# Four graph layers in one kernel: later layers' weights prepared in the second stage, constants made first, first-stage blocks waiting for nodes only

## The chip, the cores and the metric

The kernel runs on one core of a Trainium2 chip. The metric is the device time of one execution in microseconds (us). Every engine of the core works through its own instruction list in order: TensorE (PE, with its weight loads shown apart as PEld), VectorE (DVE), ScalarE (ACT), GpSimd (POOL), and SyncE (SP), whose list issues most of the transfers.

## What is computed

The input is `x`, 128 graphs of 128 nodes with 128 channels, and `adj`, a 0/1 matrix of each graph. Four layers follow one another, each `x = x + layer(relu(layernorm(x)), adj)`. The first layer decides the order of the work:

```
D = jnp.abs(x[:, :, None, :] - x[:, None, :, :])        # every pair of nodes
h = jnp.einsum('bijc,oc->bijo', D, W1) + b1
m = jnp.mean(h, axis=(0, 1, 2)); v = jnp.mean((h - m) ** 2, axis=(0, 1, 2))
h = leaky((h - m) / jnp.sqrt(v + EPS) * g1 + be1)       # then W2, mask, softmax, y, its own norm
```

The mean and variance run over all pairs of all graphs, so they must be known before any edge score can be finished. Layers 1 to 3 are attention layers over the same graphs, with weights of their own (`L1_gnn_*`, `L2_gnn_*`, `L3_gnn_*`); products of these weights (`fw`, `w2g`, `aq`, `aqb`, `a1bc`, `vpw`, `pb_bc` and some masks) are prepared once.

## The kernel before, in words

There are three stages. **First stage**, `statistics()`: for every pair of nodes of every graph it forms |difference|, multiplies by W1 and sums the results and their squares. **Second stage**, `edge_attention()`: it computes the edge scores of the neighbours only, softmax and `y` for 32 groups of four graphs. **Third stage**, `layers()`: the other three layers, group by group.

The first stage treats 32 groups of four graphs. `nodes(g)` (from L613) loads a group (L618), normalises it (DVE L623/L624, ACT L628/L629, POOL L632/L633), transposes it (PE L638), applies relu into `he` (ACT L641), copies a few columns (POOL L644) and then makes `us` (PE L653, ACT L656/L660, DVE L658/L662), three bf16 parts of W1 times the nodes. A graph is cut into four blocks, `block(b, q)` (from L687): a tile `d` of 32 x 64 pairs is made by DVE (L701) or POOL (L706), ACT takes its absolute value (L710), PE multiplies it with W1 (L727), and the result is reduced by DVE (L739) or by ACT (L733). Two of a group's sixteen blocks, called larger, take a maximum in place of the difference, need no ACT step, and add on PE three products of `us` with a constant tile `both`. Nine `d` buffers and three PSUM buffers `ph` are shared by all.

The constants and the later layers' weights are prepared in generators that run among the first blocks: `own_and_later` makes `both` (POOL L590, DVE L595), `first_weight` the transposed W1 (`w1T`, `w1T2`), `attention_weights` `fw` (L323 to L329), `w2g` (L337 to L340) and small masks (L342 to L364), `square_weights` `vpw` and `pb_row` (L385 to L389), `aT` (DVE L398), `aq` (PE L404, ACT L408) and `aqb` (PE L412, DVE L414), and `edge_constants` the constants of the second stage (POOL L419/L423, DVE L429 to L452). Their inputs are loaded by SP near the start (L282 to L299).

Nothing in the two stages runs in the order of the text. Each generator announces its next step with an engine, a cost and the buffers it takes:

```
yield "after", ("nodes", g)
yield DVE, 0.33, "", "ph"
```

The planner `in_order` (from L66) takes the makers in a list, keeps at most eight of them under way in the first stage and nine in the second, and picks the step that can begin first by its own clock. What it picks becomes the fixed instruction order of PE, ACT, DVE and POOL. `begun` gives the clocks at which the engines are thought to begin. A step after `"wait"` becomes due that much later, one after `"after"` when an event is done. In this kernel `("nodes", g)` is announced after `us`, so that no block of a group is placed before the group's `us`.

Of the kernel before, what the change touches and what calls it, by code (L numbers as in the profile page):

```python
# [19 lines left out]
P = 128  # L20
# [153 lines left out]
def kernel(ctx: ExitStack, tc: tile.TileContext, x, adj, w, out):  # L174
# [108 lines left out]
    a1b = w_tile("a1b", [P, NH, 2 * DH])  # L283
    nc.sync.dma_start(a1b, bcast(w["L1_gnn_a1"], 0, P))
    nc.sync.dma_start(w2g[:, :, 0:P], w["L1_gnn_W2"].rearrange("(s k) c -> k s c", k=P))
    a2b = w_tile("a2b", [P, 2, P])
    nc.sync.dma_start(a2b, bcast(w["L1_gnn_a2"].rearrange("(s c) -> s c", s=2), 0, P))
    araw = w_tile("araw", [P, P, NT])
    nc.sync.dma_start(araw, w["L3_gnn_a"])
    raw("qw", w["L3_gnn_qw"], nc.sync)  # L290
    raw("vw", w["L3_gnn_vw"], nc.sync)
    acol = w_tile("acol", [P, 1])
    nc.sync.dma_start(acol, w["L2_gnn_a1"])
# [24 lines left out]
    far = mid_of("far", [P, 1])  # L318

    def attention_weights():  # L320
        yield "wait", 20.0
        yield DVE, 2.9, "", ""
        nc.vector.memset(fw, 0.0)  # L323
        for m in range(2):
            prod = wl.tile([P, NH, DH], F32, tag="prod", name="prod", bufs=2)
            nc.vector.tensor_tensor(prod, w1c, a1b[:, :, m * DH : (m + 1) * DH], ALU.mult)
            sums = wl.tile([P, 2, HH], F32, tag="wsums", name="wsums", bufs=2)
            nc.vector.tensor_reduce(sums.rearrange("p s h -> p (s h)"), prod, AX.X, ALU.add)
            nc.vector.tensor_copy(  # L329
                fw[:, :, 3 * HH * m : 3 * HH * (m + 1)].rearrange("p s (k h) -> p s k h", h=HH),  # L330
                bcast(sums, 2, 3),
            )
        yield "wait", 3.0
        yield DVE, 1.9, "", ""
        for s in range(2):
            prod2 = wl.tile([P, 2, P], F32, tag="prod2", name="prod2", bufs=2)
            nc.vector.tensor_tensor(prod2, w2g[:, :, 0:P], bcast(a2b[:, s, :], 1, 2), ALU.mult)  # L337
            gw = wl.tile([P, 2], F32, tag="gw", name="gw", bufs=2)
            nc.vector.tensor_reduce(gw, prod2, AX.X, ALU.add)
            nc.vector.tensor_copy(w2g[:, :, P + s], gw)  # L340
        yield DVE, 1.3, "", ""
        nc.vector.tensor_scalar(ident_far, ident, FAR, None, ALU.mult)  # L342
        of_32 = w_tile("of_32", [P, 32])
        nc.vector.tensor_reduce(of_32, ident.rearrange("p (g k) -> p k g", k=32), AX.X, ALU.add)
        for m, dst in ((0, of_f1), (1, of_f2)):
            rows = of_32[:, 3 * HH * m : 3 * HH * (m + 1)]
            nc.vector.tensor_reduce(
                dst[:, 0:HH], rows.rearrange("p (k h) -> p h k", h=HH), AX.X, ALU.add
            )
            nc.vector.tensor_reduce(dst[:, HH : HH + 1], rows, AX.X, ALU.add)  # L350
        of_part = w_tile("of_part", [P, 3])
# [7 lines left out]
        yield DVE, 0.8, "", ""  # L359
        nc.vector.tensor_copy(a1bc, acol.to_broadcast([P, P]))  # L360
        hid = w_tile("hid", [P, P])
        nc.vector.tensor_scalar(hid, ident, 0.5, None, ALU.mult)
        for s in range(2):
            nc.vector.tensor_tensor(  # L364
                q_avg[:, s * 64 : s * 64 + 64], hid[:, 0:64], hid[:, 64:128], ALU.add
            )

    def square_weights(psum2):
        yield "wait", 8.0
# [8 lines left out]
        yield "wait", 12.0  # L378
# [5 lines left out]
        yield DVE, 0.7, "", ""  # L384
        nc.vector.tensor_copy(vpw, pvw)  # L385
        nc.vector.tensor_tensor(pb_row, pb_row, pvb, ALU.add)
        nc.vector.tensor_scalar(pb_row, pb_row, -2.0, None, ALU.add)
        ones_row = w_tile("ones_row", [1, P])
        nc.vector.memset(ones_row, 1.0)  # L389
# [5 lines left out]
        aT = w_tile("aT", [P, NT, P])  # L395
        for t in range(0, NT, 2):
            yield DVE, 0.32, "", ""
            nc.vector.tensor_copy(  # L398
                aT[:, t : t + 2, :], araw[:, :, t : t + 2].rearrange("d e t -> d t e")
            )  # L400
        yield PE, 2.1, "ph", ""
        pq = psum2("aq_ps")
        for s in range(2):
            nc.tensor.matmul(  # L404
                pq[:, s, :], raws["qw"], aT[:, 4 * s : 4 * s + 4, :], start=True, stop=True
            )
        yield ACT, 1.1, "", "ph"
        nc.scalar.copy(aq.rearrange("p t e -> p (t e)"), pq.rearrange("p s n -> p (s n)"))  # L408
        yield PE, 2.0, "ph", ""
        pqb = psum2("aqb_ps")[:, 0, 0:NT]  # L410
        for t in range(NT):
            nc.tensor.matmul(pqb[:, t : t + 1], aT[:, t, :], qb, start=True, stop=True)  # L412
        yield DVE, 0.2, "", "ph"
        nc.vector.tensor_copy(aqb, pqb)  # L414

    def edge_constants():
        yield "wait", 30.0
        yield POOL, 0.6, "", ""
        nc.gpsimd.iota(  # L419
            off, pattern=[[1, P]], base=0, channel_multiplier=-1,  # L420
            allow_small_or_imprecise_dtypes=True,
        )
        nc.gpsimd.iota(  # L423
            at, pattern=[[1, P]], base=0, channel_multiplier=0,
            allow_small_or_imprecise_dtypes=True,
        )
        yield DVE, 1.5, "", ""
        tmp = w_tile("tmp", [P, P])
        nc.vector.tensor_scalar(tmp, off, 64.0, None, ALU.is_le)  # L429
        nc.vector.scalar_tensor_tensor(tmp, off, 1.0, tmp, ALU.is_ge, ALU.mult)  # L430
        nc.vector.scalar_tensor_tensor(in_half, off, -65.0, tmp, ALU.is_le, ALU.add)
        nc.vector.tensor_scalar(tmp, ident, -1.0, 1.0, ALU.mult, ALU.add)
        nc.vector.tensor_tensor(in_other, tmp, in_half, ALU.subtract)
        nc.vector.tensor_copy(not_own, tmp)
        yield DVE, 1.3, "", ""
        nc.vector.tensor_scalar(upto, off, 0.0, None, ALU.is_ge)
        back = w_tile("back", [P, P])
        nc.vector.tensor_scalar(back, at, -1.0, P - 1.0, ALU.mult, ALU.add)
        nc.vector.tensor_tensor(tmp, back, ident, ALU.mult)
        nc.vector.tensor_reduce(down, tmp, AX.X, ALU.add)  # L440
        nc.vector.tensor_copy(down_d, tmp)
        yield DVE, 1.1, "", ""
        nc.vector.tensor_copy(ident_h, ident)
        nc.vector.memset(ones, 1.0)
        nc.vector.memset(all_p, float(P))
        nc.vector.tensor_scalar(ident5, ident, 5.0, None, ALU.mult)
        nc.vector.tensor_scalar(ident4, ident, -4.0, None, ALU.mult)
        yield DVE, 1.0, "", ""
        nc.vector.tensor_scalar(least, at[:, 0 : len(SLOTS)], float(P), float(P), ALU.mult, ALU.add)
        for k, n in enumerate(SLOTS):  # L450
            nc.vector.memset(room[:, k : k + 1], float(n))
        nc.vector.memset(far, NEG)  # L452
# [113 lines left out]
    def statistics():  # L566
# [3 lines left out]
        with tc.tile_pool(name="a2", bufs=2) as a2, tc.tile_pool(  # L570
# [17 lines left out]
            def own_and_later():  # L588
                yield POOL, 3.9, "", ""
                nc.gpsimd.tensor_tensor(  # L590
                    both.rearrange("p (i j) -> p i j", j=64),
                    shifted(ident[:, 1:65], QR), bcast(ident[:, 0:QR], 2, 64), ALU.add,
                )
                yield DVE, 0.68, "", ""
                nc.vector.tensor_scalar(both, both, -1.0, None, ALU.mult)  # L595
                yield "done", "both"

            def first_weight():
                yield "wait", 4.0
# [9 lines left out]
            def nodes(g):  # L609

                b0 = g * GB
                if g < len(raw_x):
                    xg = raw_x[g]  # L613
                    yield "wait", 4.0 + 1.2 * g
                else:
                    yield DMA, 0.6, "xg", ""
                    xg = a2.tile([P, GB, P], F32, tag="xg", name="xg")
                    nc.sync.dma_start(xg, x_t[:, b0 : b0 + GB, :])  # L618
# [27 lines left out]

                if g == 0:
# [15 lines left out]
                ready[g] = he, pt, us  # L663
                yield "done", ("nodes", g)
# [17 lines left out]
            def block(b, q):  # L682
# [11 lines left out]
                he, pt, us = ready[g]  # L694
                hb, hp, us = he[:, i, :], pt[:, i, :], us[:, :, i, :]
# [12 lines left out]
                if not is_larger:  # L708
# [4 lines left out]
                    )  # L713
                yield PE, 3.17 if is_larger else 1.76, "ph", "d"
                ph = a_ph.tile([P, 2, 512], F32, tag="ph", name="ph")
# [25 lines left out]
            ready, left, six = {}, [GB] * n_parts, {}  # L741
# [3 lines left out]
            def others():  # L745
                yield "fork", own_and_later()
                yield "fork", first_weight()
                yield "fork", attention_weights()
# [4 lines left out]
            makers = [partial(nodes, 0), others]  # L753
# [5 lines left out]
            begun = dict.fromkeys(AFTER, 1.0) | {POOL: 1.5, ACT: 5.0, DMA: 22.0}  # L759
# [67 lines left out]
    def edge_attention(free_at, banks, total):  # L827
# [3 lines left out]
        with tc.tile_pool(name="b2", bufs=2) as b2p, tc.tile_pool(name="b3", bufs=B_W) as b3p, tc.tile_pool(  # L831
            name="b_ps", bufs=6, space=PSUM
        ) as b_ps, tc.tile_pool(name="b_pq", bufs=1, space=PSUM) as b_pq:
# [336 lines left out]
            makers = [partial(total, psum, own_d), *(partial(group, g) for g in range(n_parts))]  # L1170
# [1340 lines left out]
```

## Time and profile before

| what | value |
|---|---|
| median of 3 runs | 2699.19 us (2699.1 to 2699.64) |
| profiled execution, its own time | 2704.5 us |
| its span | 2702.7 us |
| DVE begins the second stage (L770) | 1101.6 us after the span's start |
| second stage's last group | 1759.0 us |
| mean granted TensorE clock | 0.965 |

| busy over the span | PE | PEld | DVE | ACT | POOL |
|---|---|---|---|---|---|
| us | 2498.0 | 1558.9 | 2437.8 | 2160.7 | 1632.8 |
| share | 92% | 58% | 90% | 80% | 60% |

Shares over the span mix three stages with different limits, so they are read by stretches of time. A line of the timeline gives start, duration, engine, source line, operation, output and inputs with their shapes, how many instructions were merged, and in brackets the idle time before with what ended it. A line of the stretches gives its length, then the busy time of PE, PEld, DVE, ACT and POOL with the number of instructions, the granted TensorE clock, the busy share of the DMA engines and GB/s.

### The profile page before, as it was taken

The numbers are of one execution on the slowest core, as the hardware profiler recorded it, in microseconds if no ns is written. First come the engines' busy times: TensorE is split into PE (matmuls) and PEld (weight loads), VectorE is DVE, ScalarE is ACT, GpSimd is POOL, SyncE is SP. The second block draws the span as 40 slices with busy tenths as digits, with TensorE's granted clock in tenths as the row PEclk, the third lists the DMA queues.
The fourth block names the chain that finished last, engine by engine and source line by source line (L and its number), as shares of the span: only waits on it lengthen the run. The fifth ranks groups of instructions, "written<-read, shape, count | busy, mean of one in ns | idle before, by whom it ended". The sixth has DMA issues, their size and how long they took to land.

```text
span 2702.7 us, 51582 instructions
## 1 busy us (share of the span) xinstructions
PE 2498.0 (92%) x19584; PEld 1558.9 (58%) x19595; DVE 2437.8 (90%) x4648; ACT 2160.7 (80%) x3527; POOL 1632.8 (60%) x923
## 2 busy tenths in 40 slices
PE   6999999999999999799999999868988989898888
PEld 2333444333433333477777777756776767667666
DVE  7999999999999999788899998678988888889886
ACT  4899999999999999566666666568787877787885
POOL 6899999999999999644344444022433333323234
PEclk8999999999999999899999999979999999999999
DMA  3100000000000000322223321040211111111001
GB/s 88 32 24 24 24 24 24 30 26 24 24 24 28 24 20 8 102 88 91 85 85 101 93 81 50 17 137 5 62 36 47 37 44 44 45 38 31 10 2 33
DMA packets 135732, 122.62 MB, mean 45 GB/s; under 512 B 10866, under 2 KB 102451, under 8 KB 135475
## 3 DMA queue, kind: packets, MB, share of 16 engines
q1 hardware_dynamic: 134754, 118.89, 14.4%
q8 instruction: 158, 2.59, 0.4%
q14 instruction: 100, 0.81, 0.1%
q10 hardware_dynamic: 720, 0.33, 0.0%
HBM read 73.05 MB, written 46.14 MB: 44 GB/s over the span
## 4 chain that ended last, share of the span: by engine, by line
PE 45%; DVE 30%; ACT 14%; issue 6%; POOL 2%; DMA 1%; SPq 0%; ACTq 0%; DVEq 0%; POOLq 0%
PE ph L727 13%; DVE d L701 6%; ACT d L710 6%; DVE six L739 5%; PE pl L1056 4%; PE diff L1001 4%; DVE p L1752 3%; PE ph L1014 2%; PE sp L1024 2%; PE po L1709 2%; ACT ph L733 2%; PE va L1781 1%; DVE s L1640 1%; PE ph L1911 1%; PE sm L1781 1%
## 5 line engine op out<-in xcount | busy, mean ns | idle before, releaser
L706 POOL TENSOR_TENSOR d<-he 128x2016 f32<-128x2016 f32 (+1 forms) x272 | 960.7, 3564 | 14.3 <-PE ph L727 8.8
L727 PE MATMUL ph<-d,w1T 128*64 128x512 f32 (+1 forms) x4096 | 919.8, 599 | 37.7 <-DVE six L739 25.0
L710 ACT ACTIVATE d<-d 128x2048 f32<-128x2048 f32 (+1 forms) x448 | 831.8, 1888 | 21.2 <-POOL d L706 14.3
L727 PEld LDWEIGHTS ph<-d,w1T 128*64 128x64 f32 x4096 | 320.7, 137 | 566.8 <-issue 489.1
L701 DVE SCALAR_TENSOR_TENSOR d<-pt,he 128x2048 f32<-128x2048 f32 x240 | 541.5, 2270 | 1.4 <-PE ph L727 1.4
L739 DVE BATCH_NORM_STATS2 six<-ph 128x6 f32<-128x512 f32 (+1 forms) x704 | 436.1, 676 | 16.3 <-PE ph L727 15.1
L1649 POOL TENSOR_TENSOR xn<-xo,mv 128x512 f32<-128x512 f32 x64 | 74.0, 1157 | 324.0 <-DVE mv L1642 256.5
L733 ACT ACTIVATE ph<-ph 128x1008 f32<-128x1008 f32 x160 | 159.6, 997 | 20.7 <-PE ph L727 19.0
L1056 PE MATMUL pl<-its,it 128*128 128x128 f32 x1280 | 171.2, 283 | 0.5 <-DVE its L1049 0.4
L1056 PEld LDWEIGHTS pl<-its,it 128*128 128x128 f32 x1280 | 157.0, 196 | 17.8 <-DVE its L1049 5.8
L1010 ACT ACTIVATE d<-diff 128x640 f32<-128x640 f32 x128 | 89.8, 702 | 91.0 <-PE diff L1001 91.0
L1752 DVE SCALAR_TENSOR_TENSOR p<-z,mask 128x1024 f32<-128x1024 f32 x124 | 147.7, 1210 | 8.0 <-ACT z L1750 7.7
L988 POOL TENSOR_TENSOR base<-base,own_d 128x512 f32<-128x512 f32 x32 | 42.7, 1334 | 179.8 <-PE ph L1014 124.0
L1650 POOL TENSOR_TENSOR xn<-xn,rs 128x512 f32<-128x512 f32 x96 | 111.0, 1156 | 52.9 <-ACT rs L1646 40.8
L1001 PE MATMUL diff<-inc,h 128*128 128x320 bf16 x768 | 128.8, 304 | 3.9 <-DVE inc L917 3.9
L1750 ACT ACTIVATE z<-z 128x1024 f32<-128x1024 f32 x128 | 129.0, 1008 | 4.1
L1046 ACT CAST it<-pi 128x640 f32<-128x640 bf16 x128 | 86.3, 690 | 54.5 <-PE pi L1043 54.5
L917 DVE SCALAR_TENSOR_TENSOR inc<-in_row,row 128x8 bf16<-128x8 f32 (+12 forms) x512 | 126.5, 315 | 0.8 <-PE in_row L908 0.8
L1649 POOL TENSOR_TENSOR xn<-x,mv 128x512 f32<-128x512 f32 x32 | 36.1, 1129 | 136.8 <-DVE mv L1642 73.7
L1781 PE MATMUL va<-p,vals 128*32 128x128 f32 x2048 | 108.7, 285 | 8.3 <-DVE vals L1766 8.1
L1018 ACT ACTIVATE z<-ph,h_bi,h_sc 128x320 f32<-128x320 f32 x128 | 77.9, 618 | 45.0 <-PE ph L1014 43.3
L1997 POOL TENSOR_TENSOR xh<-xh,xo 128x512 f32<-128x512 f32 x32 | 46.9, 1467 | 106.6 <-DVE xh L1718 82.8
(329 smaller groups left out, 5383.9 us busy)
## 6 DMA issues: line engine op xcount, KB each, us to landing
ht<-h SPq DMA_DIRECT2D x64, 256.0 KB, 2.8
n<-ln_xn SPq DMA_DIRECT2D x32, 256.0 KB, 2.4
h<-he SPq DMA_DIRECT2D x32, 256.0 KB, 2.6
adj<-in_adj SPq DMA_DIRECT2D x32, 256.0 KB, 3.0
xn<-n SPq DMA_DIRECT2D x32, 256.0 KB, 2.8
xb<-in_x SPq DMA_DIRECT2D x32, 256.0 KB, 2.9
xb<-xb SPq DMA_DIRECT2D x32, 256.0 KB, 2.0
xg<-xb SPq DMA_DIRECT2D x32, 256.0 KB, 2.7
```

The lines of the kernel that those rows point to most:

```text
L701: nc.vector.scalar_tensor_tensor(dv, own, 0.0, later, ALU.max, ALU.max if is_larger else ALU.subtract)
L706: nc.gpsimd.tensor_tensor(dv, later, own, ALU.subtract)
L710: nc.scalar.activation(d[:, 0 : 4 * n], d[:, 0 : 4 * n], AF.Abs, accum_out=sums[:, g, k : k + 1] if on_act else None,)
L727: nc.tensor.matmul(ph[64 * a : 64 * a + 64, t, 0:n], wt, x_, start=part == 0, stop=not is_larger or part == 3,)
L733: nc.scalar.activation(ph[:, :, 0:n], ph[:, :, 0:n], AF.Square, accum_out=squares[:, g, k : k + 1])
L739: nc.vector.bn_stats(six[g][:, 2 * by_bn.index((i, q)) + t, :], ph[:, t, 0:n])
L917: nc.vector.scalar_tensor_tensor(inc[:, :, e : e + n], in_row[:, :, 0:n], float(k + 1), row[:, :, 0:n], ALU.is_equal, ALU.subtract,)
L1001: nc.tensor.matmul(diff[:, a, 0 : SLOT_N // 2], h[:, i, :], inc[:, a * SLOT_N // 2 : (a + 1) * SLOT_N // 2], start=m == 0, stop=m == 2,)
L1056: nc.tensor.matmul(made["pl"][:, i, :], it[:, k, :], its[:, k, :], start=k == 0, stop=k == 4)
L1750: nc.scalar.activation(z, z, AF.Exp, scale=1.0 - SLOPE)
L1752: nc.vector.scalar_tensor_tensor(p, z, 1.0, bcast(mask[:, i, :], 1, NH), ALU.max, ALU.mult)
L1781: nc.tensor.matmul(to[rows, a, s, :], vals[:, NH * a + e, :] if to is va else es[:, i, e : e + 1].to_broadcast([P, DH]), ps_[i][:, e, :], ...
```

## The change

Three things are done. First, `attention_weights` and the `aT`, `aq`, `aqb` part of `square_weights` become one generator, `layer_weights`, which is placed after 20 of the 32 group makers of the second stage; its steps are cut into smaller ones, its loads (`araw`, `qw`, `a1b`, `acol`, `a2b`) move there too, and four large tiles share two buffers. Second, the constants are placed first: `others` stands ahead of `nodes(0)`, many memsets and both iotas are issued before the planner, scaled copies of the identity and three more copies go to ACT, and `both` is made by one DVE instruction from a negated identity rather than by POOL and DVE. Third, `("nodes", g)` is announced once `he` is complete; `("us", g)` is a second event that only the larger blocks wait for, ahead of their PE step. The estimates in `begun` and some `"wait"` values change as well.

```diff
-    a1b = w_tile("a1b", [P, NH, 2 * DH])
-    nc.sync.dma_start(a1b, bcast(w["L1_gnn_a1"], 0, P))
...
+    minus_ident = w_tile("minus_ident", [P, P])
+
+    def scaled_idents():
+        yield ACT, 0.3, "", ""
+        nc.scalar.mul(minus_ident, ident, -1.0)
+        yield "done", "minus"
+        for dst, factor in ((ident_h, 1.0), (ident5, 5.0), (ident4, -4.0)):
+            yield ACT, 0.27, "", ""
+            nc.scalar.mul(dst, ident, factor)
+        yield ACT, 0.27, "", ""
+        nc.scalar.activation(not_own, ident, AF.Identity, bias=one, scale=-1.0)
+        yield "done", "not_own"
...
+        nc.vector.tensor_scalar(back, at, -1.0, P - 1.0, ALU.mult, ALU.add)
+        yield DVE, 0.29, "", ""
+        nc.vector.tensor_tensor(tmp, back, ident, ALU.mult)
+        yield ACT, 0.27, "", ""
+        nc.scalar.copy(down_d, tmp)
...
+        nc.vector.tensor_tensor(hid, ident[:, 0:64], ident[:, 64:128], ALU.add)
+        yield ACT, 0.5, "", ""
+        for s in range(2):
+            nc.scalar.mul(q_avg[:, s * 64 : s * 64 + 64], hid, 0.5)
+
+    def layer_weights(pool, psum):
+        def big(shape):
+            return pool.tile(shape, F32, tag="big", name="big", bufs=2)
+
+        yield DMA, 0.3, "", ""
+        araw = big([P, P, NT])
+        nc.sync.dma_start(araw, w["L3_gnn_a"])
+        qw = pool.tile([P, P], F32, tag="qw", name="qw")
+        nc.sync.dma_start(qw, w["L3_gnn_qw"])
+        yield "wait", 4.0
+        aT = big([P, NT, P])
+        for t in range(0, NT, 2):
+            yield DVE, 0.4, "", ""
+            nc.vector.tensor_copy(
+                aT[:, t : t + 2, :], araw[:, :, t : t + 2].rearrange("d e t -> d t e")
+            )
+        for s in range(2):
+            yield PE, 1.05, "p", ""
+            pq = psum("aq_ps")
+            nc.tensor.matmul(pq, qw, aT[:, 4 * s : 4 * s + 4, :], start=True, stop=True)
+            yield ACT, 0.58, "", "p"
+            nc.scalar.copy(aq[:, 4 * s : 4 * s + 4, :], pq)
...
-        yield DVE, 0.7, "", ""
-        nc.vector.tensor_copy(vpw, pvw)
-        nc.vector.tensor_tensor(pb_row, pb_row, pvb, ALU.add)
-        nc.vector.tensor_scalar(pb_row, pb_row, -2.0, None, ALU.add)
-        ones_row = w_tile("ones_row", [1, P])
-        nc.vector.memset(ones_row, 1.0)
+        yield ACT, 0.28, "", ""
+        nc.scalar.copy(vpw, pvw)
+        yield DVE, 0.3, "", ""
+        nc.vector.scalar_tensor_tensor(pb_row, pvb, -2.0, pb_row, ALU.add, ALU.add)
...
             def own_and_later():
-                yield POOL, 3.9, "", ""
-                nc.gpsimd.tensor_tensor(
+                yield "after", "minus"
+                yield DVE, 2.3, "", ""
+                nc.vector.tensor_tensor(
                     both.rearrange("p (i j) -> p i j", j=64),
-                    shifted(ident[:, 1:65], QR), bcast(ident[:, 0:QR], 2, 64), ALU.add,
+                    shifted(minus_ident[:, 1:65], QR), bcast(minus_ident[:, 0:QR], 2, 64), ALU.add,
                 )
-                yield DVE, 0.68, "", ""
-                nc.vector.tensor_scalar(both, both, -1.0, None, ALU.mult)
...
+                ready[g] = he, pt
+                yield "done", ("nodes", g)
...
-                ready[g] = he, pt, us
-                yield "done", ("nodes", g)
+                parts_of[g] = us
+                yield "done", ("us", g)
...
+                yield "after", ("us" if is_larger else "nodes", g)
+                if g == 0:
+                    yield "after", "w1"
                 yield PE, 3.17 if is_larger else 1.76, "ph", "d"
...
-            makers = [partial(nodes, 0), others]
+            makers = [others, partial(nodes, 0)]
...
-            begun = dict.fromkeys(AFTER, 1.0) | {POOL: 1.5, ACT: 5.0, DMA: 22.0}
+            begun = dict.fromkeys(AFTER, 1.0) | {POOL: 1.9, ACT: 1.8, DVE: 1.6, DMA: 22.0}
...
+            groups = [partial(group, g) for g in range(n_parts)]
+            weights = partial(layer_weights, w_late, psum)
+            makers = [partial(total, psum, own_d), *groups[:20], weights, *groups[20:]]
```

The rest of `layer_weights` holds the former instructions for `fw`, `w2g`, `a1bc`, `ident_far`, `of_f1`, `of_f2` and `parts_m`, each group behind a smaller `yield DVE`; `a1b` and `a2b` are loaded by SP just ahead of their use.

## The prediction

> **What bounds the kernel now.** I read the stretches of the span first, to find a stage that is not full, then the timeline of DVE and POOL there, then the waits. Stretches (length, then PE, PEld, DVE, ACT, POOL, clock):
>
> ```profile
> 0.00:100.00 100.00, 71.65 (x303) 30.22 (x305) 84.37 (x164) 55.20 (x65) 66.78 (x34) 0.86 0.26 73
> 100.00:1085.00 985.00, 965.56 (x4892) 386.40 (x4890) 971.59 (x1201) 964.21 (x1011) 967.26 (x343) 1.00 0.08 24
> 1400.00:1550.00 150.00, 148.29 (x1324) 116.16 (x1324) 137.38 (x360) 99.78 (x214) 64.45 (x60) 1.00 0.29 90
> ```
>
> From 100 us to the end of the first stage four engines are 98 to 99% busy: no edit to one engine's work there can gain much. The first 100 us are another matter: POOL is busy for 67 of them, ACT for 55. In the second stage PE sets the pace (98.9%), with DVE at 92% and POOL at 43%.
>
> Timeline of DVE, then of POOL, in the poor stretch:
>
> ```profile
> 20.55 3.02 DVE L326 TENSOR_TENSOR prod<-w1c,a1b 128x256 f32<-128x256 f32 x1
> 24.05 2.95 DVE L329 COPY fw<-wsums 128x24 f32<-128x24 f32 x1
> 26.92 0.41 DVE L326 TENSOR_TENSOR prod<-w1c,a1b 128x256 f32<-128x256 f32 x1
> 27.82 2.95 DVE L329 COPY fw<-wsums 128x24 f32<-128x24 f32 x1
> 38.96 2.94 DVE L340 COPY w2g<-gw 128x2 f32<-128x2 f32 x1
> 42.72 3.53 DVE L340 COPY w2g<-gw 128x2 f32<-128x2 f32 x1
> 47.56 0.15 DVE L357 COPY parts_m<-of_part 128x1 f32<-128x1 f32 x1
> ```
> ```profile
> 12.71 18.03 POOL L706 TENSOR_TENSOR d<-he 128x2016 f32<-128x2016 f32 x5
> 31.09 10.79 POOL L706 TENSOR_TENSOR d<-he 128x2016 f32<-128x2016 f32 x3
> 42.67 3.55 POOL L706 TENSOR_TENSOR d<-he 128x2016 f32<-128x2016 f32 x1 [0.79 <-PE ph L727]
> 75.45 1.04 POOL L632 TENSOR_TENSOR ln_xn<-xg,ln_mv 128x512 f32<-128x512 f32 x1 [29.23 <-DVE ln_mv L624]
> ```
>
> A copy of 2 columns takes 3.5 us on DVE, and one of 1 column 0.15 us at 47.6, when POOL is idle. POOL's five tiles of 3.6 us end near 23.5, 27.1 and 30.7; the slow DVE operations end there too, and at 41.9 and 46.2. So DVE stands behind whole POOL instructions while it makes weights that the first stage never reads. Between 20.5 and 62.1 it makes four difference tiles. The waits up to 60 us, and from 60 us on, show who pays:
>
> ```profile
> PE ph L727 <- DVE six L739: 11.8, 2, 6.9
> ```
> ```profile
> POOL ln_xn L632 <- DVE ln_mv L624: 29.2, 1, 29.2
> ```
>
> PE waits for DVE to free `ph`; POOL waits 29.2 us in one piece for the statistics of group 2, which stand on DVE behind the setup.
>
> **Part 1, setup out of the first stage.** Setup on DVE between its first difference tile (15.75) and 100 us: 10.2 (20.5 to 30.8, `fw`), 1.7 (33.1 to 34.8, `vpw`, `pb_row`), 12.2 (37.0 to 49.1, `w2g`, masks, `aT`), 1.8 + 1.0 + 0.6 + 0.4 (constants) and 0.2: 28.1 us; with the 2.3 us that it waits for PE's `aqb` product, 30.4. DVE leaves the first stage at 1101.6, so first tile to end is 1085.9 us; without the setup, and with 0.3 for the one `pb_row` instruction that stays, 1055.8. Where this stall goes, nothing else is late: the tiles are POOL's, ACT's and PE's own work, all nearly full afterwards. Counted on POOL: 29.2 of wait and 0.5 for the iotas go. The two counts agree on 29 to 30 us, because both engines stood in one queue; they are not added.
>
> **Part 2, the start with constants ahead.** Before, the statistics of group 0 began at 4.0, DVE's first tile was at 15.75 and POOL's at 12.7. In the changed instruction order `both` stands on DVE ahead of these statistics and waits for ACT's negated identity, and ACT issues its five weight loads until 4.8 first. So: identity 5.1; `both` 2.3 (nearest row: DVE L701, 2048 columns, 2.27) to 7.4; `w1T2` and `in_half` 0.5; statistics of groups 0 and 1, 1.7 each, and `upto` 0.2, to 11.4; POOL's four normalising steps of 1.04 from 9.6 to 13.8; `he` copy 0.4; POOL's first tile at 14.2, 1.4 later than now. That is the price of a step moved off a POOL that had nothing else to do (3.6 us from 1.39) onto DVE. On DVE six more constants (1.5 us) stand ahead of the first tile. Five of them can be blocked by POOL (part 4); two waits of 0.85 behind its 1.04 steps give 11.4 + 1.5 + 1.7 = 14.6, the low end. The last, `hid`, may meet POOL's first tile: 14.6 + 3.6 = 18.2, the high end. I take 16, nearer the low end, since four of the five meet steps of 1.04. `q_avg` on ACT follows `hid` and stands ahead of group 1's `he`; the same 3.6 bounds that. Five scaled identities on ACT (0.27 each) end near 6.2, under `both`. SP loses four issues of 0.43 ahead of the first `xg`; those loads are wanted 50 us later.
>
> End of the first stage: on DVE 16 + 1055.8 = 1071.8; on POOL 1101.6 - 29.7 + 1.4 = 1073.3. I take 1072.5: **29 us gained**. From both sides: 38 if the first tile comes at 14.6 and a third of the 13 to 20 us of small idle times after 100 us goes too; 20 if it comes at 18.2 and the four engines need 6 us more to fill one another's queues.
>
> **Part 3, nodes only.** In the changed order, from group 3 on, the last `us` step still stands on DVE just ahead of that group's first difference tile, and `us` begins on PE 11 to 13 blocks ahead of the first larger block, as it does now from group 4 on. The event frees the first group only; two tiles of it stand ahead of the last `us` step. Cost 0, with the rival below as the other end.
>
> **Part 4, weights in the second stage.** PE: two `aq` products were 2.5 us at 54 us (clock 0.74 there), sixteen `aqb` passes 1.95; with the faster clock 1.00, 4 us, on the engine that sets this stage. DVE, at durations with POOL idle: `aT` 4 x 0.38, `fw` and `w2g` 4 x (0.41 + 0.42 + 0.15), masks 1.8, `a1bc`, `aqb`, memset 0.5: 7.7 us, spread over groups 12 to 19, 134 us at 19.15 us a group, where DVE idles 8.4%, 11 us. ACT's two copies (1.0) lie in its 33% of idle time. SP: five loads; `a1b` and `a2b` wait for a `big` buffer, and stores and prefetches stand behind them; inputs are three groups ahead, so 0, and a few us if a buffer comes late. The first, `araw`, stands behind a wait for PE in the first stage, ahead of group 4's load, which is not due for 50 us: 0.
>
> Here a rule speaks against the change. Row first: DVE L1080, two inputs from SBUF in this stage, has a median of 0.70 and a mean of 1.16. The Trainium skill, page "SBUF — State Buffer", section "Who interferes with whom", says that a DVE instruction with two SBUF inputs, or a copy in a two-port mode, shares a port pair with GpSimd, and whoever comes second waits for the whole instruction of the other. That fits the 2.95 us copies, and the move does not escape it: 17 of the moved instructions are of these kinds. By the rule at its worst each waits a whole POOL step of this stage (L988, 1.33): 22.6 us. By the rows the mean excess of L1080, L904, L944 and L1068 is 0.46, 0.22, 0.27 and 0.20, on average 0.29: 4.9 us. I take the rows, since these operations meet the same POOL. DVE then has 12.6 us more in 11 us of idle time; idle time is not all usable, and I let 3 us reach PE. **Second stage: +7**; ends +3 (all hidden, PE fills its own 1.1% of idle time) and +24 (4 on PE, 30 less 11 on DVE, rounded up).
>
> **Sum.** Against the profiled execution: 2704.5 - 29 + 7 = 2682.5. It is 5.3 us above the median of the runs (2699.2), so 2677.2 there; I say **2677**.
>
> **Rivals.** *The weights hide completely and the start fills at once*: 38 - 3 = 35 gained, 2664. For it: the second stage's POOL is often idle for 15 us. Against: DVE at 92% is close to full. *The start stays poor*: DVE's blocked constants, and a TensorE that drops to clock 0.50 when starved, as from 30 to 40 us now; 14 gained, 12 paid: 2697 at worst, 2690 as I see it. Against: after `hid` DVE's steps in this stage read one input from SBUF at most. *Everything comes back in the second stage* by the rule's worst price: -29 + 24, 2694, about no change. *Slower*: blocks placed before their parts. PE takes its list in order; if at each of 31 group changes the larger block waits for `us` (its chain took 3.5 us in the first group), two `d` buffers and two engines wait with it. At 1.2 us a change this is 37 us: 2677 + 37 = 2714. It decides from 0.9 us a change (28 us). Against it: the 11 to 13 blocks of distance, over 20 us.
>
> **Chances.** Forecast (2668 to 2686) 0.62; complete hiding 0.18; poor start 0.10; all back 0.05; slower 0.05. A run of this kernel can tell about 0.2%, 5.4 us, from no change: faster 0.90, same 0.05, slower 0.05. The range from 2661 to 2690 takes in the bounds of start and second stage and leaves out most of the last two.
>
> **What would show it.** DVE begins the second stage near 1072; POOL's wait of 29 us is gone, its first tile at 14.2 and DVE's at 14.6 to 18.2; in the first 100 us POOL is busy for over 90. The second stage, from DVE's first step in it to its last group, is 657.4 us now (1101.6 to 1759.0) and should be near 664. The sum is wrong if POOL and DVE wait for each other in the first 40 us, if PE waits for `us` at group changes, or if the moved DVE steps average over 1 us more than here.

## The result, and the profile after

| | before | after |
|---|---|---|
| median | 2699.41 us (2695.72 to 2701.21, 6 runs) | 2676.66 us (2673.85 to 2680.34, 6 runs) |
| profiled execution, its own time | 2704.5 us | 2677.98 us |
| DVE begins the second stage | 1101.6 us | 1070.3 us |
| second stage, to its last group | 657.4 us | 662.1 us |
| from there to the end of the span | 943.7 us | 943.7 us |

The ratio is 0.9917 [0.9904, 0.993]: the kernel is 0.8% faster. In the traces the first stage is 31.3 us shorter and the second 4.7 us longer, which is 26.6 us in all; in the medians 22.8. The difference is that the profiled execution of before lies 5 us above its runs and that of after only 1.3. All stage times below are from single profiled executions and carry such a few us; verdicts are from medians.

The stretches after (length, then PE, PEld, DVE, ACT, POOL, clock):

```profile
0.00:100.00 100.00, 85.89 (x423) 36.62 (x425) 94.85 (x155) 87.24 (x104) 90.95 (x43) 1.00 0.26 77
100.00:1060.00 960.00, 945.90 (x4780) 382.67 (x4778) 942.48 (x1172) 936.01 (x987) 940.35 (x333) 1.00 0.08 23
1400.00:1550.00 150.00, 147.59 (x1295) 116.24 (x1296) 129.90 (x344) 95.62 (x201) 70.39 (x64) 0.99 0.30 92
```

The first 100 us are no longer poor: POOL goes from 66.8 to 91, ACT from 55 to 87, PE from 72 to 86 and the clock from 0.86 to 1.00. The rest of the first stage is as full as it was. POOL's difference tiles at the start, and its wait of group 2:

```profile
14.37 3.55 POOL L727 TENSOR_TENSOR d<-he 128x2016 f32<-128x2016 f32 x1
18.22 35.22 POOL L727 TENSOR_TENSOR d<-he 128x2016 f32<-128x2016 f32 x10
55.52 7.07 POOL L727 TENSOR_TENSOR d<-he 128x2016 f32<-128x2016 f32 x2
```
```profile
POOL ln_xn L651 <- DVE ln_mv L643: 7.9, 1, 7.9
```

POOL makes ten tiles in one row; before, its rows were of five, three and one, and then it waited for 29 us. Its one wait for statistics up to 60 us is the 7.9 us at the very start, for group 0. Where the weights are made now, in the second stage, DVE's timeline has the copies that took 2.9 to 3.5 us before:

```profile
1472.46 0.18 DVE L412 COPY fw<-sums 128x24 f32<-128x24 f32 x1
1473.87 0.18 DVE L412 COPY fw<-sums 128x24 f32<-128x24 f32 x1
1480.21 1.37 DVE L423 TENSOR_TENSOR big<-w2g,big 128x256 f32<-128x256 f32 x1
...
1482.07 0.17 DVE L426 COPY w2g<-gw 128x2 f32<-128x2 f32 x1
```

They take 0.17 and 0.18 us. One of the products (0.41 alone) met a POOL step and took 1.37. The second stage as a whole, before and after:

```profile
1101.60:1759.00 657.40, 627.00 (x5479) 489.80 (x5486) 571.99 (x1466) 408.68 (x868) 270.02 (x248) 0.97 0.25 79
```
```profile
1070.30:1732.40 662.10, 631.01 (x5508) 490.79 (x5514) 577.59 (x1495) 411.55 (x872) 275.16 (x251) 0.98 0.26 80
```

PE is busy 4.0 us longer and idle 0.7 us longer: that is the whole 4.7.

### The profile page after: what moved, and what is told of

It is laid out like the page before. It is cut to its first block, busy times and chain, and to the rows that moved or that the text cites. A ratio compares the mean times of both kernels' runs of the same rounds, so it can differ in the third digit from the quotient of the medians.

```text
span 2676.1 us, 51543 instructions
## 1 busy us (share of the span) xinstructions
PE 2489.0 (93%) x19585; PEld 1559.4 (58%) x19595; DVE 2423.4 (91%) x4638; ACT 2160.1 (81%) x3537; POOL 1632.1 (61%) x922
## 3 DMA queue, kind: packets, MB, share of 16 engines
q1 hardware_dynamic: 134754, 118.89, 14.6%
## 5 line engine op out<-in xcount | busy, mean ns | idle before, releaser
L727 POOL TENSOR_TENSOR d<-he 128x2016 f32<-128x2016 f32 (+1 forms) x272 | 961.0, 3560 | 17.7 <-PE ph L752 14.2
L764 DVE BATCH_NORM_STATS2 six<-ph 128x6 f32<-128x512 f32 (+1 forms) x704 | 438.0, 677 | 11.7 <-PE ph L752 11.4
L1076 DVE TENSOR_TENSOR its<-pi,s 128x640 f32<-128x640 bf16 x128 | 102.2, 809 | 13.1 <-ACT it L1073 12.7
```

Of the source, the lines that this page charges most:

```text
L727: nc.gpsimd.tensor_tensor(dv, later, own, ALU.subtract)
L764: nc.vector.bn_stats(six[g][:, 2 * by_bn.index((i, q)) + t, :], ph[:, t, 0:n])
```

## The experiments

My theory after the result: DVE's short operations in the first stage cost what is left of a POOL tile each, so the gain is the setup that left POOL's tile stream; it adds up by parts, most of it from the weights. Rivals: the gain is the nodes-only event's, or the cost sits in certain operations (the four copies). Runs of before beside these experiments have medians of 2701.66 to 2703.09 us, so kernels are compared by their ratios to before.

### The three parts, one at a time and in pairs

**Only the weights moved** (the kernel before with `layer_weights` in the second stage; the constants and their order stay; `hidden` is what is left of the old generator, `hid` and `q_avg`):

```diff
-                yield "fork", attention_weights()
+                yield "fork", hidden()
...
+            makers = [partial(total, psum, own_d), *groups[:20], weights, *groups[20:]]
```

> The kernel before, with the later layers' weights prepared in the second stage and nothing else changed (both on POOL, constants among the first blocks, blocks wait for us). Theory (DVE's setup queue starves the first stage): about 22 of the 28.1 us of setup and the 2.3 us wait for aqb leave the first stage, so DVE begins the second stage 22 to 25 us earlier than 1101.6, the second stage is 5 longer, net 17 to 20 us faster than before, about 2681. Rival (the constants placed first, or the earlier event, did the work): at most 6 us faster. Rival (only the planner's new packing): no prediction better than 0 to 25 either way, and the 29 us wait of POOL for group 2's statistics would stay.

Measured: 2705.56 us, ratio 1.0015 [1.0008, 1.0022], so no gain; if anything it is slightly slower. The theory that the parts add falls here. DVE's timeline shows why:

```profile
20.45 2.89 DVE L394 TENSOR_SCALAR hid<-ident 128x128 f32<-128x128 f32 x1
23.37 6.98 DVE L396 TENSOR_TENSOR q_avg<-hid 128x64 f32<-128x64 f32 x2
...
47.82 3.46 DVE L444 TENSOR_SCALAR tmp<-ident 128x128 f32<-128x128 f32 x1
51.31 3.54 DVE L445 TENSOR_TENSOR in_other<-tmp,in_half 128x128 bf16<-128x128 f32 x1
54.78 3.56 DVE L446 CAST not_own<-tmp 128x128 bf16<-128x128 f32 x1
```

These same constants took 0.22, 0.36 for the two, 0.23, 0.29 and 0.22 us before, at 48 to 52 us, when POOL stood idle. With the weights gone, `hid` and `q_avg` come 25 to 28 us earlier and meet POOL's first row of five tiles (12.69 to 30.27); the others meet a row of three (47.55 to 58.27), where POOL had nothing to do before.

**Only the weights stay** (the changed kernel with `layer_weights` among the first stage's setup):

```diff
-            makers = [partial(total, psum, own_d), *groups[:20], weights, *groups[20:]]
+            makers = [partial(total, psum, own_d), *groups]
...
+                yield "fork", layer_weights(wl, psum1)
```

> The changed kernel, but with the weights prepared in the first stage, from the same generator. Theory: the constants' 4 us are gone from the middle of the first stage and the second stage is 5 us shorter than in the changed kernel, but DVE stands behind POOL's tiles for the weights again, 20 to 25 us; 3 to 10 us faster than before, about 2693. Rival (constants first or the earlier event did the work): 2676 or better, since the second stage is relieved of 5 us.

Measured: 2697.82 us, 0.9984 [0.9978, 0.9991], inside what was expected. The weights' copies are dear again:

```profile
69.57 2.96 DVE L412 COPY fw<-sums 128x24 f32<-128x24 f32 x1
...
88.14 2.94 DVE L426 COPY w2g<-gw 128x2 f32<-128x2 f32 x1
```

**The event after `us`** (the changed kernel, `("nodes", g)` announced last, as before):

```diff
-                ready[g] = he, pt
-                yield "done", ("nodes", g)
...
                 yield "done", ("us", g)
+                ready[g] = he, pt
+                yield "done", ("nodes", g)
```

> The changed kernel with the event for nodes announced after us, as before. Theory (the event frees the first group only, some two tiles): within 4 us of the changed kernel, 2676 to 2680. Rival (the earlier event carries the gain): 8 us or more slower than the changed kernel, with PE or DVE waiting at the start of groups.

Measured: 2688.28 us, 0.9953 [0.9939, 0.9966]: without its event the change loses about 10 us (0.0036 of 2700), more than I gave it and within what the rival had (8 us or more). The first difference tile on DVE comes late, since `us` of group 0 stands ahead of it:

```profile
16.97 0.43 DVE L677 TENSOR_TENSOR pu<-pu,us 128x256 f32<-128x256 f32 x1 [2.72 <-ACT us L675]
...
19.01 2.28 DVE L722 SCALAR_TENSOR_TENSOR d<-pt,he 128x2048 f32<-128x2048 f32 x1
```

In after this tile is at 14.29, 4.7 us earlier. The first stage ends 9.5 us later here, so about 5 us are lost further on. DVE's waits over the first stage, of this kernel and then of after, show most of them:

```profile
DVE six L764 <- PE ph L752: 17.6, 26, 4.9
DVE pu L677 <- ACT us L675: 3.4, 3, 2.7
```
```profile
DVE six L764 <- PE ph L752: 11.4, 19, 2.4
...
DVE pu L679 <- ACT us L677: 0.5, 1, 0.5
```

**The event alone** and **weights and event** (the kernel before, and the first experiment's, with the event announced when `he` is complete):

```diff
+                ready[g] = he, pt
+                yield "done", ("nodes", g)
...
-                yield PE, 3.17 if is_larger else 1.76, "ph", "d"
+                yield "after", ("us" if is_larger else "nodes", g)
+                if g == 0:
+                    yield "after", "w1"
+                yield PE, 3.17 if is_larger else 1.76, "ph", "d"
```

> The kernel before, with one part of the change: a block of the first stage waits for its nodes, and only a first-row block for their parts. If the parts of the change add, this takes off what the same edit is worth on top of the other two, about 11 us: near 2690. If the price is the stall of DVE's short operations behind POOL's tiles, POOL's earlier tiles only make more of the setup meet a tile, and little is left: 2696 to 2703, with the setup's copies and constants dearer in the trace than before.

> The kernel before with two parts of the change, the later layers' weights in the second stage and blocks that wait for nodes only; the constants stay where they were, among POOL's tiles. If the parts add, 2705.6 less 11: near 2694. If the constants alone are enough to stall DVE behind POOL's tiles, 2697 to 2705; what is left to the whole change (2677) is then what placing the constants ahead of POOL's tiles is worth, 20 us or more.

Measured: 2695.3 us, 0.9974 [0.9963, 0.9984], and 2698.66 us, 0.9985 [0.9978, 0.9992]. The event alone is worth about 7 us, between its two expectations, and the setup is not dearer with it (29.0 us against 29.9, table below), so the second of them misses its sign too. Its first difference tile on DVE is at 10.26 instead of 15.75, which is most of the 6.4 us that the first stage gains. With the weights moved as well, the rest of the constants stalls DVE, as the second expectation of that run has it (what is left to the whole change is 18 us by the ratios, where 20 or more was expected): `q_avg` again (its two instructions 6.98 us), and now others:

```profile
38.18 3.58 DVE L442 SCALAR_TENSOR_TENSOR tmp<-off,tmp 128x128 f32<-128x128 f32 x1
...
45.34 3.45 DVE L444 TENSOR_SCALAR tmp<-ident 128x128 f32<-128x128 f32 x1
```

Together these runs separate two terms. "Setup" counts DVE's setup instructions that begin after 12.7 us and adds the durations of their timeline rows (16 short memsets of `room` are one row); busy and idle are DVE's, from 0 to its first step in the second stage. W is the weights moved, C the constants ahead (with the estimates in `begun` and the `"wait"` values that belong to them), E the event (C and E: only the weights stay; W and C: the event after `us`).

| parts | ratio of medians | first stage ends | DVE busy | DVE idle | setup on DVE |
|---|---|---|---|---|---|
| none | 1 | 1101.6 | 1065.7 | 35.9 | 70 in 29.9 us |
| W | 1.0015 | 1099.9 | 1062.8 | 37.1 | 41 in 24.8 |
| E | 0.9974 | 1095.2 | 1064.7 | 30.5 | 70 in 29.0 |
| W and E | 0.9985 | 1088.0 | 1061.9 | 26.1 | 41 in 24.8 |
| C and E | 0.9984 | 1096.2 | 1069.3 | 26.9 | 34 in 28.7 |
| W and C | 0.9953 | 1079.9 | 1046.1 | 33.8 | 5 in 1.9 |
| all | 0.9917 | 1070.3 | 1044.8 | 25.5 | 5 in 1.9 |

The last column is the answer. With 29 or 36 of the 70 instructions gone, the setup still takes DVE 25 to 29 us: while any are left in POOL's stream of tiles, they take over the stalls of those that left. Only W and C together empty the stream, and only then does DVE's busy time fall, by 20 to 21 us against before. (It falls by less than the 28 us of the column, since in the whole change DVE is busy for 8.4 us ahead of 12.7 us, before for 4.0.) The four rows with E show it in the times: with neither 0.9974, with W 0.9985, with C 0.9984, with both 0.9917. The event acts on another column: it takes 5.4, 11.0 and 8.3 us off DVE's idle time, added to nothing, to W, and to W and C. C alone was not tried.

### Is it POOL's tiles, and does it matter which operation?

**Four short copies on ACT** (the kernel before):

```diff
-            nc.vector.tensor_copy(
+            nc.scalar.copy(
                 fw[:, :, 3 * HH * m : 3 * HH * (m + 1)].rearrange("p s (k h) -> p s k h", h=HH),
...
-            nc.vector.tensor_copy(w2g[:, :, P + s], gw)
+            nc.scalar.copy(w2g[:, :, P + s], gw)
```

> The kernel before, with only the four short copies into fw and w2g (L329, L340: 2.95, 2.95, 2.94 and 3.53 us on DVE) made by ACT. Theory (a copy on DVE stands behind a whole POOL instruction, and this stall is part of what starves the stage): ACT makes each in under 0.3 us, DVE gets 11 us back, unless the next operation of that kind meets POOL in its place; 6 to 11 us faster than before. Rival (these copies are slow by themselves, in any engine): ACT shows 2 us or more for each. Rival (amount of setup matters, not the stall): within 3 us of before.

Measured: 2699.99 us, 0.9999 [0.999, 1.0007], no change, although DVE lost the four instructions that took 12.4 us in the trace of before. On ACT the four take 0.19 to 0.21 us each, so they are not slow by themselves. The time is what the last rival asked for, within 3 us, but the stall did not vanish: DVE's setup takes only 0.7 us less in all, because the next in line took the copies' place:

```profile
23.95 3.32 DVE L326 TENSOR_TENSOR prod<-w1c,a1b 128x256 f32<-128x256 f32 x1
...
39.00 3.29 DVE L398 COPY aT<-araw 128x256 f32<-128x256 f32 x1
42.21 3.58 DVE L342 TENSOR_SCALAR ident_far<-ident 128x128 bf16<-128x128 f32 x1
```

The second product took 0.41 before, the copy to `aT` 0.38 and `ident_far` 0.21.

**One copy, or one reduction, of two columns at the end of each group** (the changed kernel; the 32 added instructions make something that nobody reads):

```diff
+                    yield DVE, 0.15, "", ""
+                    nc.vector.tensor_copy(small[:, 2 * g : 2 * g + 2], two_cols)
```
```diff
+                    nc.vector.tensor_reduce(small[:, g : g + 1], two_cols, AX.X, ALU.add)
```

> The changed kernel, with one copy of two columns from SBUF to SBUF added on DVE at the end of each of the 32 groups of the first stage, into a tile that nothing reads. Each takes 0.15 us alone. Theory (what starved the first stage before were DVE operations that stand behind whole POOL tiles, whatever their size): each waits for what is left of a 3.55 us tile, 1.8 us in the mean and up to 3.6, so DVE gets 60 to 110 us more work in a stage where it has 10 us of idle time; first stage 45 to 100 us longer, 2720 to 2775. Rival (the amount of setup work decides): 5 us, 2682.

> The same, with a sum over the same two columns in place of each copy: one input[...]. Theory: no wait for POOL, 32 x 0.15 = 5 us on DVE, of which idle time hides a part; 2677 to 2683. Rival (any small operation there breaks the packing): as slow as with the copies.

Measured: 2746.18 us, 1.016 [1.0145, 1.0176], and 2676.4 us, 0.9903 [0.9888, 0.9919]: about 70 us against nothing, for the same 32 times two columns. The two groups of instructions (durations in ns, least, median, greatest):

```profile
L706 DVE COPY small<-two_cols x32: 105/2529/3358, 59.2 to 1144.0; 128x2 f32<-128x2 f32 x32
```
```profile
L706 DVE TENSOR_REDUCE small<-two_cols x32: 98/147/154, 60.5 to 1072.4; 128x1 f32<-128x2 f32 x32
```

Of the 32 copies, 31 end 22 to 30 ns after the POOL instruction that was under way when they began; the last, with POOL idle, takes 0.105 us. One of them, with its tile (1047.65 + 3.55 = 1051.20):

```profile
1047.65 3.55 POOL L732 TENSOR_TENSOR d<-he 128x2016 f32<-128x2016 f32 x1
1048.37 2.86 DVE L706 COPY small<-two_cols 128x2 f32<-128x2 f32 x1
```

The first stage ends at 1144.0 and 1072.4, 71.6 us apart. The copies add 63.0 us on DVE (1.97 in the mean) and the reductions 4.6; DVE also idles 12 us longer with the copies (38.4 against 26.2). So in this full stage the whole stall goes to the end, and some idle time on top.

### The price in the second stage, and the start

**Weights prepared twice** (the changed kernel, after 12 and after 20 groups; the second time makes the same values again):

```diff
-            makers = [partial(total, psum, own_d), *groups[:20], weights, *groups[20:]]
+            makers = [
+                partial(total, psum, own_d), *groups[:12], weights, *groups[12:20], weights, *groups[20:]
+            ]
```

> The changed kernel, with all of the later layers' weights prepared twice in the second stage (after 12 and after 20 group makers; the second time writes the same values). Theory: once cost 4.7 us by the two traces (662.1 against 657.4 us), of which 4 are PE's; twice 4 to 7 us more, 2681 to 2684. Rival (waits for POOL dominate the price there): 12 to 24 us more. Rival (4.7 was packing, and the weights are hidden): within 2 us.

Measured: 2691.59 us, 0.9962 [0.9948, 0.9975], 12 to 15 us above after. The size is what the rival with the waits for POOL gave, not its reason: the short copies are not blocked (medians 0.18 and 0.17 us), and both sets take DVE 21.5 us together where one took 11.7 in after. Nor is 4 us of PE enough, so the main expectation fell too. In the trace the stage grows by 21.7 us (and the rest of the span is 5.4 shorter): PE is busy for 646.9 us (15.9 more) at a mean clock of 0.96, and idle for 5.8 more. A stretch of 50 us inside the second set:

```profile
1469.00:1519.00 50.00, 46.78 (x397) 37.24 (x394) 40.85 (x109) 28.77 (x61) 18.17 (x16) 0.92 0.27 83
```

PE is idle for 3.2 of 50 us, and its clock is 0.92; at the same place of the stage after has 49.95 busy at 1.00. Nearly all of it is one gap of 3.05 us:

```profile
1507.01 1.37 DVE L423 TENSOR_TENSOR big<-w2g,big 128x256 f32<-128x256 f32 x1
...
1510.40 0.36 DVE L423 TENSOR_TENSOR big<-w2g,big 128x256 f32<-128x256 f32 x1
...
1512.29 2.47 PE L1083 MATMUL pl<-its,it 128*128 128x128 f32 x10 [3.05 <-DVE its L1076]
```

The two products, reductions and copies for `w2g` stand on DVE ahead of the `its` that PE waits for, 3.3 us of work in all, the first product behind a POOL step; by these rows it was their place in DVE's order that opened the gap. From 1513 to 1521 PE is then busy without a pause, at a clock of 0.50. The second set's own passes are 4 of the 15.9 us more, so by estimate about 12 are longer passes at a lower clock; what the other gaps cost stays open.

**Weights after 28 groups**, alone and **with the negated identity on DVE**:

```diff
-            makers = [partial(total, psum, own_d), *groups[:20], weights, *groups[20:]]
+            makers = [partial(total, psum, own_d), *groups[:28], weights, *groups[28:]]
```

> The changed kernel with the weights begun after 28 makers of the second stage instead of 20, nearer its end, where PE has spare time and POOL little work. If the weights cost the second stage their own 4.7 us where they lie, most of that comes back: 2672 to 2675. If the order that the planner finds decides, anything from 2673 to 2684, with no sign that can be told beforehand.

> The changed kernel with the weights after 28 makers, and with the negative identity made by VectorE, so that the tile of both signs doesn't wait for ScalarE. The start is 3 us earlier in the trace, as it was with that edit alone, where none of the 3 us reached the end. If start and second stage add: 2670 to 2674. If the planner's packing takes back what the start gives: as weights_late, within 2 us.

Measured: 2703.15 us, 1.0007 [0.9998, 1.0015], and 2705.03 us, 1.0006 [0.9997, 1.0014]. Moved by eight groups, the weights cost the whole gain of the change; both expectations for the first run fell, and the second run is within 2 us of it, as its rival had it. The first stage ends at 1068.9, 1.4 us earlier than in after, and the second takes 684.6 us, 22.5 more: PE is idle 14.0 more and busy 8.5 more. Near its end:

```profile
1672.00:1686.00 14.00, 13.69 (x123) 10.27 (x120) 10.33 (x22) 8.37 (x20) 0.00 (x0) 1.00 0.06 20
1686.00:1700.00 14.00, 4.13 (x15) 1.65 (x17) 13.65 (x42) 0.70 (x1) 0.00 (x0) 0.61 0.00 1
```
```profile
1679.89 0.39 PE L935 MATMUL in_row<-row,ranks 128*128 128x128 bf16 x4
...
1691.05 0.58 PE L935 MATMUL in_row<-row,ranks 128*128 128x128 bf16 x4 [3.76 <-DVE row L931]
```

In the second of these stretches PE is busy for 4.1 of 14 us, while DVE works off the last groups' edge lists and the degree counts all together; the same matmuls take 0.58 us where they took 0.39, the mean clock being 0.61. Up to the 28th group, a group's `ranks`, an early step of its edge list, come within 3.3 us of where they do in before, counted from the stage's start; the 29th are 25 us late, and the last come at 620.1 against 588.0 in before and 602.3 in after. After shows such delays too, from the 21st group on (up to 26 us), but its last group ends only 4.7 us later than in before, where here it ends 27 us later. That the weights' generator holds one of the nine places under way for 129 us (1529.0 to 1657.8), just when the last groups should start, fits this, but it is argued and not shown.

**The negated identity on DVE** (the changed kernel):

```diff
-        yield ACT, 0.3, "", ""
-        nc.scalar.mul(minus_ident, ident, -1.0)
+        yield DVE, 0.22, "", ""
+        nc.vector.tensor_scalar(minus_ident, ident, -1.0, None, ALU.mult)
...
                 nc.scalar.copy(w1T, pw[:, 0, 0:64])
+                yield "wait", 4.0
```

> The changed kernel, with the negated identity made by DVE rather than by ACT behind its five weight loads, and the doubled W1 placed behind the statistics of the first two groups. Theory (the start is a chain: negated identity, both, statistics of group 0, normalising on POOL, first tile): both begins near 2 in place of 5.3, POOL's first tile at 11.2 in place of 14.4, 3 us faster than the changed kernel, near 2674. Rival (the planner's packing moves by more than that): anything within 8 us of 2677, with the first tile 3 us earlier all the same.

Measured: 2676.56 us, 0.9907 [0.9892, 0.9922], the same as after. DVE's first tile is at 11.34 instead of 14.29, yet the first stage ends only 0.5 us earlier:

```profile
0.00:100.00 100.00, 89.49 (x430) 38.12 (x432) 95.93 (x161) 87.98 (x105) 92.06 (x44) 0.98 0.26 77
```

PE has gained 3.6 us in this stretch, but DVE only 1.1 (95.93 against 94.85). What DVE no longer waits at the start it waits later: over the whole first stage it idles for 24.6 us against 25.5. An earlier first tile was worth here only what it took off that sum. No version tried beats the changed kernel.

## Why the prediction was right, and where it was not

- **The time**: 2677 against 2676.66. Against the profiled execution the sum said 2682.5 and 2678.0 was measured, 4.5 us better; taking the median of before 5.3 below its profile made up for it, since after's profile lies only 1.3 above its own median. The agreement within 1 us is partly chance.
- **What bounds it**: right. The poor stretch was the first 100 us, and the cause was DVE standing behind whole POOL tiles: 32 copies of two columns cost 70 us, 32 reductions nothing, and 31 of the copies ended with the POOL instruction under way.
- **Part 1**: "first tile to end ... 1055.8", measured 1070.33 - 14.29 = 1056.0. But this number holds for the whole change only. With weights and constants moved and no event it is 1079.85 - 19.01 = 1060.8, so Part 1 was worth 25 us, not 30, and the event supplied the rest. The way it was added up, instruction by instruction, would have priced half of the setup at half of the gain. Taking out the weights alone gained nothing (1.0015).
- **Part 2**: POOL's first tile at 14.37 (14.2), DVE's at 14.29 where 14.6 to 18.2 was given and 16 taken. `hid` took 0.41 us: it met no tile. The low end was the right one. Two readings were off without effect on the sum: between 20.5 and 62.1 the lines show three difference tiles of DVE, not four, and the steps up to the statistics' end add up to 11.5, not 11.4.
- **Part 3**: "Cost 0" is the step that failed, though not far enough to spoil the sum. The event is worth about 10 us on top of the other two. Of the 9.5 us in the trace, 4.7 lie at the first tile; Part 2 had them in its sum unnamed, because it read the start off the changed order. The other 5 are DVE's waits for PE and ACT. The text looked at whether blocks are placed ahead of their parts, which they rarely are, and not at what the planner may put in between.
- **Part 4**: 4 us on PE, measured 4.0. The 3 us allowed to reach PE were 0.7: together 4.7 against 7. The moved DVE steps took 11.7 us against 12.6, and DVE's busy time in the stage rose by 5.6. The measured rows were the right price, and the worst price, which the prediction worked out by the rule of the Trainium skill's page "SBUF — State Buffer", section "Who interferes with whom", was not paid: the four short copies of the moved weights met no POOL step, and the `aT` copies took 4.5 us together against 1.5 alone. The same section says that a reduction doesn't contend with GpSimd; the 147 ns above agree.
- **Rivals**: PE's matmuls show no wait for `us` from 60 us to the end of the first stage, and its weight loads only twelve (5.3 us in all, 0.6 at most), so the slower case didn't come. "All back in the second stage" didn't come either, but moving the weights by eight groups brings it about, with PE running dry near the stage's end. The prediction's list of what would make it wrong had no such case: it priced the place of the weights in engine time alone.

## What to carry to other kernels

Amid back-to-back GpSimd instructions, a copy, cast, scaling or two-input operation on DVE cost here what was left of the GpSimd instruction under way and not its own length. Count such operations; here removing some moved the stall to the next ones, and the gain came when the last had left. Before valuing a part of a change by a sum over instructions, ask whether what remains can take over the same wait. And where a step is put in a planned order can cost more than its engine time: after 28 of 32 groups the same weights cost 22.5 us of stage time more than after 20.

## What the runs showed of the hardware

- A copy of 2 columns on DVE among POOL tiles of 3.55 us took 2.53 us in the median and 3.36 at most; a reduction of the same columns 0.147. In this kernel not only copies waited: products, casts, scalings by a constant and a `scalar_tensor_tensor` with two inputs from SBUF (3.58 us against 0.29) did too.
- In two places a gap of 3 to 4 us on TensorE cost twice. After one of 3.05 us its granted clock was 0.50 from 1513 to 1521 us although it was busy throughout; after one of 3.76 us the same group of matmuls took 0.58 us instead of 0.39. Shorter gaps had no fixed price: in after the clock stayed at 1.00 from 1670.3 to 1690.3 us with 2.4 of 20 us idle (no gap over 1.01), and in the kernel with the weights twice it was 0.83 from 1669 to 1689 with 1.5 us idle (no gap over 0.73). No run separates what decides between the two.
